# A graph layer on one core: single-row copies taken out, and gathers that land seven to a buffer on counters of their own

## The chip, the cores and the metric

The kernel runs on one core of a Trainium2 chip. The metric is device time of one execution in microseconds (us). TensorE is called PE here, VectorE DVE, ScalarE ACT, GpSimd POOL and SyncE SP, as in the profile. The granted TensorE clock in the profiled execution was 1.000 throughout.

## The reference

There are 50,000 nodes with 128 features each and 1,650,000 edges, sorted by their destination. Each edge takes its source's row through one of two weight matrices, chosen by the edge's type, and the results are summed at the destination.

```python
Xs = X[src]
m_data = Xs @ W_data.T + b_data
m_ctrl = Xs @ W_control.T + b_control
msg = jnp.where((edge_types == 0)[:, None], m_data, m_ctrl)
agg = jax.ops.segment_sum(msg, dst, num_segments=X.shape[0])
out = agg + (X @ W_self.T + b_self)
return jax.nn.relu(out)
...
x = _layernorm(x + _L0_gnn_ref(...), axis=-1)
```

The list of edges holds one self loop per node (source = destination), 50,000 in all; the kernel makes use of that.

## The kernel before

**Order of the sums.** Rows are summed first and multiplied by the weights afterwards. For a block of edges the kernel keeps two sums of source rows per destination node, one for each edge type, in `sums` (a ring of three tiles, each for 128 destination nodes of its own block and the 128 after them). When a block is done, `layer` multiplies the sums of its 128-node window by the two message weights, adds the self term and the biases, and `moments` and `store` do the residual, the layer norm and the output.

**Blocks, steps and chunks.** The sorted edges are cut into blocks of BE = 3800 edges: 28 chunks of 128 edges (C = 28, four steps of R = 7 chunks), 4 x 22 edges that take the place of self loops in those chunks (`fill`, on DVE: a self loop needs no gather, since its row lies in the block's window, so its place in a chunk is given to another edge), and X = 128 edges whose rows are copied one at a time. There are NBLK = 435 blocks. The first has no such extras, and the last has 8 chunks.

**How a row gets to SBUF.** There are two ways.
- `products(b, q)` (line 441) issues on POOL, for each chunk, one indirect DMA that gathers 128 rows of 512 bytes (line 451) into a tile `y` of its own. The pool `gat` holds 70 of these tiles, so POOL can be up to 70 gathers (2.5 blocks) ahead of PE. PE then multiplies `y` by a 128 x 76 matrix of ones and zeros (`oh`, made on DVE by `onehot`, line 396) and so adds each row to the sum of its destination and type: two passes per chunk in float32, line 454. After the 7 chunks of a step (8 in the last step of a block) two small matmuls (line 457) add the counts, and DVE adds the step's result to `sums` (`add`, line 465).
- `single_rows(b, q)` (line 427) copies the X = 128 remaining rows of a block one by one with plain DMAs whose address is in a register: SP issues 64 of them and ACT 64, a quarter of each in each step, two blocks ahead (line 439; the registers are loaded at line 434). They land in one tile `yx`, which is the 29th chunk of the block (k == C in `products`).

**Order on the engines.** The order of all instructions is written out by hand in one Python loop over the blocks (line 520), and each engine works through its share of it in that order. The steps that matter below stand in it as follows.
- At the head of block b DVE adds the last step of block b-1 (line 465), ACT copies the half of `sums` that reaches into the new block (`take_over`, line 470), and DVE adds the left-out self loops (`add_left_out`, line 363).
- In step 1 PE computes the self loops of block b+1 (`left_out_numbers`, line 349). The one PSUM tile `pl` that it writes must have been read by line 363.
- ACT's instructions for block b are `take_over`, one square root (line 489) and the 64 row copies of block b+2, in this order. ACT therefore starts the copy of line 470 for the next block after it has issued the 64 row copies.
- `fill` (lines 297 to 326) works five blocks ahead on DVE and makes the index list `idx` for the gathers. `left_out_columns` (line 333, PE) and `left_out_matrix` (lines 340 and 341, DVE) follow it.

**Waits.** The framework adds all waits. It counts POOL's DMAs on eight counters that take turns. A gather waits until the eighth gather before it has landed, and until PE has used the tile that it overwrites. PE waits for the landing of each gather before its matmul.

If a check of the inputs at the end (lines 569 to 594) found that a step's destinations don't fit its W columns, a slow general version would run; it does not run with these inputs, before or after.

Of the kernel before, what the change touches and what calls it, by code (L numbers as in the profile page):

```python
# [14 lines left out]
U8 = mybir.dt.uint8  # L15
# [8 lines left out]
D = 128  # L24
ROW = 4 * D
# [9 lines left out]
W = 38  # L35
# [3 lines left out]
X = 128  # L39
C1 = C + 1  # L40
F = 22
BE = C * CH + Q * F + X
# [7 lines left out]
GC = GB * C1  # L50
AHEAD = 2
RAHEAD = 5
# [27 lines left out]
def straight(ctx, tc, c, x, x_t, src_t, dst_t, etype_t, src_f, dst_f, etype_f, src_x, dst_first, first_p, out):  # L80

# [18 lines left out]
    gat = ctx.enter_context(tc.tile_pool(name="gat", bufs=70))  # L100
# [49 lines left out]
    one_g = {}  # L150

    def load_edges(g):
        t = eds.tile([1, GB * X], I32, name="one_g")
        nc.sync.dma_start(t, src_x[None, g * GB * X:(g + 1) * GB * X])
        one_g[g] = t
        loads[g] = {}
        for name, a in (("s", src_t), ("d", dst_t), ("t", etype_t)):
            t = eds.tile([P, GB, C1], I32, name=name, bufs=1)
            nc.sync.dma_start(t.rearrange("p b c -> p (b c)"), a[:, g * GC:(g + 1) * GC])
            loads[g][name] = t  # L160
        for name, a in (("sf", src_f), ("df", dst_f), ("tf", etype_f)):
            t = eds.tile([GS, F], I32, name=name, bufs=1)
            nc.sync.dma_start(t, a[g * GS:(g + 1) * GS, :])
            loads[g][name] = t
# [69 lines left out]
    def columns(g):  # L234
# [5 lines left out]
        def first_of(rel, d):  # L240
            yield (rel[:, :, :C].rearrange(steps, r=R), d[:, :, :C].rearrange(steps, r=R),
                   first[:, :, :, None].to_broadcast([P, GB, Q, R]))
            yield rel[:, :, C:], d[:, :, C:], first[:, :, Q - 1:]

        def first_of_f(rel, d):
# [6 lines left out]
        nc.vector.tensor_tensor(h[:, :, :, :R], a["s"][:, :, :C].rearrange(steps, r=R),  # L252
                                a["d"][:, :, :C].rearrange(steps, r=R), op=ALU.is_equal)
# [15 lines left out]
        nc.vector.tensor_scalar(cb, a["t"][:, :, :C], 0.0, float(P), op0=ALU.not_equal, op1=ALU.mult)  # L269
        nc.vector.tensor_tensor(cb, cb, a["d"][:, :, :C], op=ALU.add)  # L270
# [11 lines left out]
        nc.vector.scalar_tensor_tensor(stay, rk, F - LOOP, v[:, :, :C], op0=ALU.is_ge, op1=ALU.mult)  # L282
# [14 lines left out]
    def fill(b):  # L297
# [21 lines left out]
        nc.vector.scalar_tensor_tensor(col_g[g][:, i, :C], idx, -float(P), vi, op0=ALU.mult, op1=ALU.add)  # L319
# [45 lines left out]
    def chunks_of(b, q):  # L365

        n = C1 if not plain(b) else C if b == 0 else RCH if b < NBLK else 0
        return range(q * R, max(q * R, min((q + 1) * R if q < Q - 1 else C1, n)))
# [7 lines left out]
    bys, pcs, zs, pls = {}, {}, {}, {}  # L376
    ats = {}
    ohs, cnts, ys, accs, xws, xTs, pos, hs, mvs, sds = {}, {}, {}, {}, {}, {}, {}, {}, {}, {}
# [5 lines left out]
    def window(b):  # L384
        at = base_of(b)
        xw = stp.tile([B, D], F32, name="xw", bufs=5)
        nc.sync.dma_start(xw, x[bass.ds(at, B), :])
        xT = stp.tile([P, B], F32, name="xT", bufs=5)
        nc.sync.dma_start(xT, x_t[:, bass.ds(at, B)])
        xws[b], xTs[b] = xw, xT  # L390

    def onehot(b):
        g, i = divmod(b, GB)
        n = C1 if not plain(b) else C if b == 0 else RCH
        oh = ohp.tile([P, C1, 2 * W], F32, name="oh")
        nc.vector.tensor_tensor(oh[:, :n, :], col_g[g][:, i, :n, None].to_broadcast([P, n, 2 * W]),  # L396
                                num_ps[:, None, :].to_broadcast([P, n, 2 * W]), op=ALU.is_equal)
        ohs[b] = oh

    def counts(b):  # L400

        cnt = ohp.tile([P, Q, 2 * W], BF16, name="cnt")
        with nc.allow_low_precision(reason="whole numbers up to R + 1"):
            whole = [q for q in range(Q) if len(chunks_of(b, q)) == R]
            n = len(whole)
            nc.vector.tensor_reduce(cnt[:, :n, :], ohs[b][:, :n * R, :].rearrange("p (q r) w -> p q w r", r=R),  # L406
                                    AX.X, ALU.add)
            for q in steps_of(b):
                if q not in whole:
                    k = chunks_of(b, q)  # L410
                    nc.vector.tensor_reduce(cnt[:, q, :], ohs[b][:, k[0]:k[-1] + 1, :].rearrange("p r w -> p w r"),  # L411
                                            AX.X, ALU.add)
        cnts[b] = cnt

    SHARE = X // 2
    TURN = SHARE // Q
    RANGE = dict(min_val=0, max_val=(N - 1) * ROW, skip_runtime_bounds_check_because="where a node's row is")
    x_bytes = x.rearrange("n d -> (n d)").bitcast(U8)[None, :]

    def offsets(b):  # L420

        if not plain(b):
            g, i = divmod(b, GB)
            ats[b] = stp.tile([1, X], I32, name="at_x", bufs=AHEAD + 2)
            nc.vector.tensor_scalar(ats[b], one_g[g][:, i * X:(i + 1) * X], float(ROW), None, op0=ALU.mult)

    def single_rows(b, q):

        if q == 0:
            ys[b] = stp.tile([X, D], F32, name="yx", bufs=AHEAD + 2)  # L430
        both = []
        for j, (eng, dma) in enumerate(((SP, nc.sync), (ACT, nc.scalar))):
            at = j * SHARE + q * TURN
            _, rows = nc.values_load_multi_w_load_instructions(  # L434
                ats[b][0:1, at:at + TURN], engines=[eng], **RANGE)
            both.append([(dma, at + k, row) for k, row in enumerate(rows)])
        for pair in zip(*both):
            for dma, k, row in pair:
                dma.dma_start(ys[b][k:k + 1, :].bitcast(U8), x_bytes[:, bass.ds(row, ROW)])  # L439

    def products(b, q):
        g, i = divmod(b, GB)
        acc = ps.tile([P, 3, W], F32, name="acc")
        ks = chunks_of(b, q)
        for k in ks:
            if k == C:
                r, y = X, ys.pop(b)
            else:
                r = LAST if b == NBLK - 1 and k == RCH - 1 else P
                y = gat.tile([P, D], F32, name="y")  # L450
                nc.gpsimd.indirect_dma_start(  # L451
                    out=y[:r], out_offset=None, in_=x,
                    in_offset=bass.IndirectOffsetOnAxis(ap=idxs[b][:r, k:k + 1], axis=0))
            nc.tensor.matmul(acc[:, :2, :].rearrange("p t w -> p (t w)"), y[:r], ohs[b][:r, k, :],  # L454
                             start=k == ks[0], stop=k == ks[-1])
# [36 lines left out]
    def store(b):  # L492
# [5 lines left out]
        nc.sync.dma_start(out[bass.ds(base_of(b), B), :], o)  # L498

    for b in range(1, AHEAD + 1):  # L500
        offsets(b)
# [7 lines left out]
    for b in range(1, RAHEAD):  # L509
# [3 lines left out]
        if b < AHEAD:  # L513
            onehot(b)
            counts(b)
            for q in range(Q):
                single_rows(b, q)
        if b == 1:
            clear_sums()
    for b in range(NBLK + 1):  # L520
# [16 lines left out]
        for q in range(Q):  # L537
# [24 lines left out]
            if q == 3:  # L562
                left_out_matrix(b + RAHEAD)
                offsets(b + AHEAD + 1)
            if not plain(b + AHEAD):
                single_rows(b + AHEAD, q)
# [252 lines left out]
def gnn_resnorm(  # L819
# [10 lines left out]
    src_x: bass.AP,  # L830
# [39 lines left out]
    with ExitStack() as own:  # L870
        straight(own, tc, c, x, x_t, src_t, dst_t, etype_t, src_f, dst_f, etype_f, src_x,
# [57 lines left out]
```

## Time and profile before

| | before |
|---|---|
| median of 10 runs | 22197.53 us (22146.84 to 22237.11) |
| profiled execution, time | 22200.31 us |
| profiled execution, span | 22198.3 us |
| PE busy, matmuls | 7101.0 us (32%) |
| DVE busy | 6982.5 us (31%) |
| ACT busy | 353.7 us (2%) |
| POOL busy | 11493.4 us (52%) |
| gathers on POOL (line 451) | 12160, mean 945 ns |
| row copies on SP and on ACT (line 439) | 27712 each |

Instructions that issue DMAs from SP and ACT are not counted as busy, so ACT's 2% says nothing about its queue. The idle time of an engine is put down to what ended it. A wait of which the trace doesn't show the source is called "remote", and time in which an engine waited for nothing that the trace shows is called "issue". In the timelines, "ACTq" and "SPq" stand for the queues that issue DMAs, with how many were issued in the stretch shown.

### The profile page before, as it was taken

How to read it: one execution, taken by the hardware profiler on the slowest of the kernel's cores; microseconds unless marked ns; L12 is line 12 of the kernel's file. 1: busy time of each engine (PE TensorE's matmuls, PEld its weight loads, DVE VectorE, ACT ScalarE, POOL GpSimd, SP SyncE). 2: the span in 40 equal slices, each digit the busy share in tenths (PEclk: the TensorE clock that was granted, in tenths of full speed). 3: DMA queues.
4: the chain of work that ended last, by engine and by line, in shares of the span. 5: the costliest groups of instructions: out<-in, count | busy, mean ns of one | idle time of the engine just before them, and what ended most of it. 6: DMA issues, size and time to landing. Idle time of an engine off the chain costs nothing. (4 is left out here: it accounts for less than half of the span.)

```text
span 22198.3 us, 239078 instructions
## 1 busy us (share of the span) xinstructions
PE 7101.0 (32%) x34233; PEld 6718.6 (30%) x34234; DVE 6982.5 (31%) x12861; ACT 353.7 (2%) x875; POOL 11493.4 (52%) x12170
## 2 busy tenths in 40 slices
PE   2333333333333333333333333333333333333333
PEld 2233323333323232323333332233332332332323
DVE  3333333333333333333333333333333333333332
ACT  0000000000000000000000000000000000000000
POOL 5555555555555555555555555555555555555554
DMA  1111111111111111111111111111111111111111
GB/s 47 44 44 44 43 44 44 45 44 44 44 43 44 44 44 44 44 43 45 44 44 43 44 43 44 43 44 43 43 44 43 44 43 44 43 43 44 43 43 37
DMA packets 724493, 968.72 MB, mean 44 GB/s; under 512 B 282786, under 2 KB 522533, under 8 KB 722896
## 3 DMA queue, kind: packets, MB, share of 16 engines
q0 software_dynamic: 389120, 797.69, 13.8%
q1 hardware_dynamic: 277914, 141.12, 2.4%
q10 hardware_dynamic: 55862, 14.50, 0.3%
q14 instruction: 1314, 10.76, 0.2%
q8 instruction: 283, 4.64, 0.1%
HBM read 923.55 MB, written 28.66 MB: 43 GB/s over the span
## 5 line engine op out<-in xcount | busy, mean ns | idle before, releaser
L451 POOL DMA_INDIRECT y<-in_x,idx x12152 | 11484.3, 945 | 10606.6 <-PE acc L454 5659.8
L454 PE MATMUL acc<-oh,y 128*128 128x76 f32 x24320 | 5524.9, 422 | 13.9 <-issue 11.3
L454 PEld LDWEIGHTS acc<-oh,y 128*128 128x128 f32 x24320 | 5365.2, 332 | 14.0 <-issue 14.0
L363 DVE TENSOR_TENSOR sums<-pl,sums 128x384 f32<-128x384 f32 x433 | 241.5, 558 | 12890.5 <-ACT sums L470 12870.6
L349 PE MATMUL pl<-z,ones_b 88*128 88x256 bf16 x433 | 171.0, 395 | 10831.4 <-DVE sums L363 10818.2
L349 PEld LDWEIGHTS <-ones_b 88*128 88x128 bf16 x433 | 45.1, 104 | 10908.8 <-DVE sums L363 10895.5
L406 DVE TENSOR_REDUCE cnt<-oh 128x228 bf16<-128x1596 f32 (+2 forms) x435 | 1278.1, 2938 | 0.1
L333 PE MATMUL small<-ones_b,by 128*88 128x1 bf16 x433 | 100.8, 233 | 3239.3 <-DVE by L326 2614.9
L333 PEld LDWEIGHTS <-by 128*88 128x88 bf16 x433 | 64.0, 148 | 3290.4 <-DVE by L326 2663.9
L396 DVE TENSOR_TENSOR oh<-col,small 128x2204 f32<-128x2204 f32 (+2 forms) x435 | 1049.8, 2413 | 0.0
L457 PEld LDWEIGHTS <-to_row 128*128 128x128 bf16 x3476 | 631.2, 193 | 31.7 <-issue 30.7
L340 DVE COPY at<-small 88x1 f32<-88x1 f32 x433 | 66.9, 155 | 1813.7 <-PE po L475 1112.6
L326 DVE TENSOR_REDUCE by<-old 128x88 bf16<-128x616 f32 x433 | 577.8, 1334 | 19.5 <-issue 1.9
L476 PE MATMUL po<-bias,sums 3*128 3x128 f32 x870 | 344.1, 496 | 701.0 <-DVE sums L465 400.0
L470 ACT COPY sums<-sums 128x384 f32 x434 | 222.2, 512 | 21049.6 <-DMA yx<-in_x 20359.5
L478 PE MATMUL po<-wmsgT,sums 128*128 128x128 f32 x1740 | 531.6, 461 | 0.0
L465 DVE TENSOR_TENSOR sums<-acc,sums 128x114 f32 x1738 | 472.3, 272 | 177.4 <-remote 39.7
L411 DVE TENSOR_REDUCE cnt<-oh 128x76 bf16<-128x608 f32 x434 | 501.4, 1155 | 0.0
L457 PE MATMUL acc<-cnt,to_row 128*128 128x38 bf16 x3476 | 480.8, 219 | 46.1 <-issue 45.4
L476 PEld LDWEIGHTS po<-bias,sums 3*128 3x128 f32 x870 | 216.0, 307 | 824.9 <-DVE sums L465 453.3
L478 PEld LDWEIGHTS po<-wmsgT,sums 128*128 128x128 f32 x1740 | 403.4, 322 | 97.6 <-issue 97.6
L307 DVE TENSOR_TENSOR m<-rk,small 128x616 f32<-128x616 f32 x433 | 344.6, 796 | 17.1 <-DVE small L305 2.4
(116 smaller groups left out, 4524.6 us busy)
## 6 DMA issues: line engine op xcount, KB each, us to landing
yx<-in_x ACTq DMA_DIRECT2D x27712, 0.5 KB
yx<-in_x SPq DMA_DIRECT2D x27712, 0.5 KB
y<-in_x,idx POOLq DMA_INDIRECT x12152
xw<-in_x SPq DMA_DIRECT2D x435, 64.0 KB
xT<-in_x_t SPq DMA_DIRECT2D x435, 64.0 KB
out<-o SPq DMA_DIRECT2D x435, 64.0 KB
vf_all<-vd SPq DMA_DIRECT2D x44, 440.0 KB
s<-in_src_t SPq DMA_DIRECT2D x44, 145.0 KB
```

The costliest lines, as they stand in the source:

```text
L307: nc.vector.tensor_tensor(m, rk_g[g][:, i, :, None].to_broadcast([P, C, F]), rank_no_ps[:, None, :].to_broadcast([P, C, F]), op=ALU.is_equal)
L326: nc.vector.tensor_reduce(by, old.rearrange("p (q r) f -> p q f r", r=R), AX.X, ALU.add)
L363: nc.vector.tensor_tensor(part, pls.pop(b)[:, :, :B], part, op=ALU.add)
L396: nc.vector.tensor_tensor(oh[:, :n, :], col_g[g][:, i, :n, None].to_broadcast([P, n, 2 * W]), num_ps[:, None, :].to_broadcast([P, n, 2 * W ...
L406: nc.vector.tensor_reduce(cnt[:, :n, :], ohs[b][:, :n * R, :].rearrange("p (q r) w -> p q w r", r=R), AX.X, ALU.add)
L411: nc.vector.tensor_reduce(cnt[:, q, :], ohs[b][:, k[0]:k[-1] + 1, :].rearrange("p r w -> p w r"), AX.X, ALU.add)
L451: nc.gpsimd.indirect_dma_start(out=y[:r], out_offset=None, in_=x, in_offset=bass.IndirectOffsetOnAxis(ap=idxs[b][:r, k:k + 1], axis=0))
L454: nc.tensor.matmul(acc[:, :2, :].rearrange("p t w -> p (t w)"), y[:r], ohs[b][:r, k, :], start=k == ks[0], stop=k == ks[-1])
L457: nc.tensor.matmul(acc[:, 2, :], to_row[:, t, :], cnts[b][:, q, t * W:(t + 1) * W], start=t == 0, stop=t == 1)
L465: nc.vector.tensor_tensor(part, accs.pop((b, q)), part, op=ALU.add)
L476: nc.tensor.matmul(po, a[0:3, 2, :B], bias, start=False, stop=False)
L478: nc.tensor.matmul(po, a[:, t, :B], c["wmsgT"][:, t * D:(t + 1) * D], start=False, stop=t == 1)
```

## The change

The single rows go. A block has BE = 28 x 128 + 88 = 3672 edges, the number of blocks becomes 450, the last with 11 chunks, and the number of gathers goes from 12160 to 448 x 28 + 28 + 11 = 12583. The functions `offsets` and `single_rows`, the lists of single rows and their loads go with them. W goes from 38 to 36, so that `oh` has 28 x 72 numbers per partition in place of 29 x 76.

The gathers of a step go into one tile `y` of seven slots. The pool has ten of these tiles, so the room is 70 gathers as before. Each tile has a completion counter of its own. The framework's eight counters are not used for these gathers, and PE waits once per step, until all seven have landed. The address for the output of a block is no longer loaded a second time (`bases`).

```diff
-W = 38
+W = 36
-X = 128
-C1 = C + 1
-BE = C * CH + Q * F + X
+BE = C * CH + Q * F
+SLOTS = 10
...
-    gat = ctx.enter_context(tc.tile_pool(name="gat", bufs=70))
+    gat = ctx.enter_context(tc.tile_pool(name="gat", bufs=SLOTS))
...
-    def offsets(b):
...
-    def single_rows(b, q):
...
+    landed = [tc.alloc_semaphore(f"landed{i}") for i in range(SLOTS)]
+    seen = [0] * SLOTS
+    step_no = [0]
+
+    def gathers(b, q):
+        ks = chunks_of(b, q)
+        i = step_no[0] % SLOTS
+        step_no[0] += 1
+        y = gat.tile([P, R, D], F32, name="y")
+        for k in ks:
+            r = LAST if b == NBLK - 1 and k == RCH - 1 else P
+            copy = nc.gpsimd.indirect_dma_start(
+                out=y[:r, k - ks[0], :], out_offset=None, in_=x,
+                in_offset=bass.IndirectOffsetOnAxis(ap=idxs[b][:r, k:k + 1], axis=0))
+            copy.then_inc(landed[i], 16)
+            tc.no_tile_sem_insts.add(copy.ins.name)
+            tc.add_to_no_dep_group(f"rows{b}_{q}", copy.ins)
+        seen[i] += 16 * len(ks)
+        wait = nc.tensor.wait_ge(landed[i], seen[i])
+        tc.declare_fence(wait.ins, group=f"rows{b}_{q}")
+        return y
 
     def products(b, q):
+        y = gathers(b, q)
...
-            if k == C:
-                r, y = X, ys.pop(b)
-            else:
-                r = LAST if b == NBLK - 1 and k == RCH - 1 else P
-                y = gat.tile([P, D], F32, name="y")
-                nc.gpsimd.indirect_dma_start(
-                    out=y[:r], out_offset=None, in_=x,
-                    in_offset=bass.IndirectOffsetOnAxis(ap=idxs[b][:r, k:k + 1], axis=0))
-            nc.tensor.matmul(acc[:, :2, :].rearrange("p t w -> p (t w)"), y[:r], ohs[b][:r, k, :],
+            r = LAST if b == NBLK - 1 and k == RCH - 1 else P
+            nc.tensor.matmul(acc[:, :2, :].rearrange("p t w -> p (t w)"), y[:r, k - ks[0], :], ohs[b][:r, k, :],
                              start=k == ks[0], stop=k == ks[-1])
...
-        nc.sync.dma_start(out[bass.ds(base_of(b), B), :], o)
+        nc.sync.dma_start(out[bass.ds(bases.pop(b), B), :], o)
...
-                offsets(b + AHEAD + 1)
-            if not plain(b + AHEAD):
-                single_rows(b + AHEAD, q)
```

## The prediction

> **What bounds the kernel now.** I read the page first. It shows no engine near full: POOL leads with 52%, and nearly half of its span is idle. The costliest group is the gather.
>
> ```profile
> POOL 5555555555555555555555555555555555555554
> L451 POOL DMA_INDIRECT y<-in_x,idx x12152 | 11484.3, 945 | 10606.6 <-PE acc L454 5659.8
> yx<-in_x ACTq DMA_DIRECT2D x27712, 0.5 KB
> ```
>
> The load is the same from end to end, so one block stands for all: 22198.3 / 435 = 51.03 us. Next I read the list of waits, which shows who holds whom.
>
> ```profile
> ACT sums L470 <- DMA yx<-in_x: 20359.5, 418, 175.6
> DVE sums L363 <- ACT sums L470: 12870.6, 432, 40.8
> PE pl L349 <- DVE sums L363: 10818.2, 431, 34.6
> POOL y L451 <- PE acc L454: 5674.1, 1326, 19.5
> POOL y L451 <- issue: 2806.7, 8949, 3.9
> POOL y L451 <- remote: 1491.6, 1281, 6.1
> ```
>
> Read it from the bottom up. POOL waits for PE's matmul of line 454 (the matmul 70 gathers back frees its tile). PE waits 25 us a block (10818.2 / 431) at line 349 for DVE's line 363, DVE waits 30 us for ACT's copy of line 470, and ACT is not waiting for data at all: it is issuing row copies. ACT's timeline says so.
>
> ```profile
> 9989.99 0.51 ACT L470 COPY sums<-sums 128x384 f32 x1 [51.28 <-DMA xw<-in_x]
> 9992.25 0.29 ACT L489 ACTIVATE sd<-mv,eps 128x1 f32<-128x1 f32 x1 [1.75 <-DVE mv L487]
> 9993.46 46.64 ACTq L439 DMA_DIRECT2D yx<-in_x  x64
> 10040.92 0.51 ACT L470 COPY sums<-sums 128x384 f32 x1 [48.38 <-DMA xw<-in_x]
> ```
>
> From one copy of line 470 to the next are 50.93 us, and 46.64 of them go into 64 row copies (0.73 us each). That is the block's period. What hangs on it is seen right after 10040.92 in the timeline of all engines:
>
> ```profile
> 10041.47 0.56 DVE L363 TENSOR_TENSOR sums<-pl,sums 128x384 f32<-128x384 f32 x1 [27.64 <-ACT sums L470]
> 10042.08 0.39 PE L349 MATMUL pl<-z,ones_b 88*128 88x256 bf16 x1 [23.29 <-DVE sums L363]
> 10042.48 3.21 PE L454 MATMUL acc<-oh,y 128*128 128x76 f32 x14
> 10043.41 0.94 POOL L451 DMA_INDIRECT y<-in_x,idx  x1 [10.87 <-PE acc L454]
> ```
>
> ACT, DVE, PE and POOL start within 2.5 us of each other. ACT's queue of row copies is the bound, and POOL is held by it through four hands. What POOL does when nobody holds it is seen at the start, where the 70 tiles are still free:
>
> ```profile
> 102.14 0.94 POOL L451 DMA_INDIRECT y<-in_x,idx  x1 [0.30 <-issue]
> 103.38 0.94 POOL L451 DMA_INDIRECT y<-in_x,idx  x1 [0.30 <-issue]
> 104.63 0.94 POOL L451 DMA_INDIRECT y<-in_x,idx  x1 [0.30 <-issue]
> 106.25 0.94 POOL L451 DMA_INDIRECT y<-in_x,idx  x1 [0.67 <-PE acc L454]
> ```
>
> One gather per 1.248 us: from 32.23 to 104.63 in the same timeline are 58 gathers in 72.40 us. The first wait for a tile comes after some 78 of them. Finally, the end of the trace, where ACT has no more rows to issue:
>
> ```profile
> 22146.73 0.51 ACT L470 COPY sums<-sums 128x384 f32 x1 [34.09 <-DMA yx<-in_x]
> 22155.55 0.51 ACT L470 COPY sums<-sums 128x384 f32 x1 [6.26 <-DVE sums L465]
> 22170.86 0.51 ACT L470 COPY sums<-sums 128x384 f32 x1 [8.89 <-DVE sums L465]
> ```
>
> The same copies are now 8.82 and 15.31 us apart, and they wait for DVE instead of the row copies.
>
> **The change part by part.**
>
> *Row copies removed.* ACT and SP lose 64 copies and their register loads in each block, ACT the 46.64 us seen above. ACT keeps 0.51 + 0.29 us of work a block, and line 470 starts as soon as DVE's line 465 is done. How soon is that? The trace has it: from line 470 to the line 465 that the next line 470 needs are 20.65 us (5009.15 to 5029.80), 22.1 (5059.69 to 5081.80), 23.6 (9989.99 to 10013.55) and 24.0 (18057.33 to 18081.30). So the loop of ACT, DVE and PE could turn in about 20 to 24 us per block. This includes DVE's wait at line 340, whose six rows sum to 1814 us or 4.2 us a block.
>
> *What is late next.* POOL. A block needs 28 gathers, and 28 x 1.2486 = 34.96 us, against 24 for the loop. (1.2486 is the mean duration 0.9450, which is 11484.3 / 12152, plus the gap of 0.3036 between two unhindered ones.) The margin is 11 us a block, and every tenth block's `columns` uses up some 6 us of it on DVE (24.4 to 30.6 in the start's timeline). PE and DVE then wait for the gathers, and the tiles that POOL wants are long free.
>
> *More blocks.* The 128 edges of each block that went by row copies go by gathers: 12583 in place of 12160. The 423 more cost 423 x 1.2486 = 528 us on the path. The 15 more blocks of DVE and PE work lie beside POOL's.
>
> *Counters of their own.* Each gather loses a wait on POOL's queue (an EVENT_SEMAPHORE of 17 ns, 12092 of them). I count nothing for it: the first of these waits is at 39.8 us, and the gathers before it stand at the same 0.30 us from each other as those after it. If POOL waits instead once a step for a tile or a counter, a bound from above is 0.2 us x 1800 steps = 360 us, worked out from the 0.12 us per gather that the "remote" waits take now (1491.6 / 12152), rounded up. Below zero I allow 0.02 us per gather, the EVENT_SEMAPHORE itself: -0.25 ms at most, in the main case nothing.
>
> *One wait of PE for seven.* PE starts a step up to six gathers (7.5 us) later than it could. Behind that wait stand the step's matmuls, then DVE's line 465. POOL is at least 60 gathers from needing those tiles, so it costs nothing but once, at the end.
>
> *W from 38 to 36, the 29th chunk gone.* DVE's `oh` and `cnt` shrink (2.42 us and 1.15 us in a block of the trace), PE saves a chunk per block. All of it lies beside POOL. SP no longer loads an address twice; SP binds nothing.
>
> *A rule weighed: sharing out descriptor work.* The row is the 46.64 us for 64 copies. The Trainium skill ("Perfetto Trace Analysis", DMA Optimizations) advises spreading DMAs over SP, ACT and GpSimd where generating descriptors is the bottleneck. By it this change is a loss: POOL takes 528 us more and nothing comes back, some 22,730 us. But the trace has 128 rows in 1.25 us on POOL and one row in 0.73 us on ACT, with the pass to the next block behind it. The rows decide; I follow them.
>
> *A second rule: DVE against POOL.* The row is the gather's mean of 945 ns with a median of 944: stretching costs about 13 us in the whole run. Some of it is at the start, where a gather took 2.41 us beside DVE's long operations. The skill ("SBUF — State Buffer", SBUF: two separate sides) says that GpSimd can't write descriptors while DVE runs an operation in a two-port mode. DVE's busy share rises from 31% to about 44% of the time, so each gather would meet more of them: its copies, casts and scalar operations come to about 1.4 us a block (lines 304, 305, 318, 340, 341, 497), at worst 450 x 1.4 = 630 us. The trace's 13 us already contain the same operations per block, so I take 15 us and keep half of the rule's figure in the range.
>
> *The sum.* Start of the first gather 8.3, stretching of the first gathers about 4, then 12583 x 1.2486 = 15,711. After the last gather comes a tail: the last product to the end took 22.4 us before (22175.9 to 22198.3), plus landing, and some 10 us because the last block is short (11 gathers, 13.7 us) and the loop of 20 us lags: 35 us. Span: 8 + 4 + 15,711 + 35 = 15,758 us. The time is 2.0 us over the span, as in the profiled execution before, whose 22200.31 is 2.8 us above the median: 15,760 us.
>
> **The rivals.**
>
> *A: POOL unheld, as above.* For it: the four hands, the first 78 gathers, the end of the trace. 15,760 us.
>
> *B: the loop of DVE, PE and ACT becomes the bound.* In the window 5009.15 to 5059.69 DVE is busy 15.43 us, PE 16.18, ACT 0.81, together 32.4; with the 4.2 us at line 340 it would be 36.6 us a block if nothing overlapped: 450 x 36.6 = 16,470 us. It decides from 34.96 us. Against it: the 20 to 24 us measured.
>
> *C: a gather waits for PE's one wait of the step before (slower).* All gathers of a step count on one tile's counter, and the fence for tile and counter is on PE. If the fence makes POOL hold the next step's first gather until PE is through with the last one, then a step is 8.74 us of gathers, about 3.3 us of matmuls and a landing. No row here shows a landing; the skill ("DMA: Bandwidth & Descriptors", Anatomy of one DMA) puts 2.0 us plus bytes over 436 GB/s, 2.15 us as an estimate. 14.2 us x 1800 = 25,560 us. It turns into a loss from 12.3 us a step (22,198 / 1800), a stall of 3.6 us. Against it: ten tiles and ten counters.
>
> *D: ACT only looks like the bound.* If POOL kept its 1.8255 us per gather (22198.3 / 12160) for another reason, 12583 of them give 22,970 us. Against it: the end of the trace.
>
> **How the numbers follow.** A 0.88, B 0.09, C 0.02, D 0.01. The time is A's, 15,760. The low end, 15,650, is A without its tail and with a third of the EVENT_SEMAPHOREs' time given back. The high end adds to A the 360 us of new waits or half of the 630, and reaches into B's lower part: 16,150. A and B are faster, C and D slower: faster 0.965, slower 0.03, and 0.005 for within 0.2%, about what a measurement of this kernel can tell from no change.
>
> **What would show it.** POOL's busy share near 75% with nearly all its idle time under "issue", a spacing of 1.25 us everywhere; ACT idle ended by DVE's line 465, not by DMAs; PE's largest wait for gathers, about 18 us a block. Wrong would be: POOL still waiting for PE for microseconds in each block (B or C; a wait in every step for C, in every block for B), or a gather clearly longer than 945 ns.

## The result: 0.813 of the time in the first measurement, and 1.028 on another chip

| | kernel before | kernel after | ratio, 95% |
|---|---|---|---|
| first measurement | 22192.25 us (28 runs) | 18051.33 us (8 runs, 18048.51 to 18053.09) | 0.8134 [0.8127, 0.8141] |
| a second chip, both kernels unchanged | 15339.33 us (7 runs, 15279.42 to 15342.36) | 15759.26 us (4 runs, 15757.71 to 15760.01) | 1.028 [1.0256, 1.0304] |

The prediction was 15,760 us and a range of 15,650 to 16,150. The first measurement is outside of it, though on the predicted side. On the second chip the predicted time came out within a microsecond, but there the kernel before is faster still, and the change is a loss. Both rows have to be explained. The experiments ran on four chips. The kernel before took 22,131 us on the first of them, within 0.4% of the profile that the prediction was made from, and 15,242 to 15,339 us on the other three. Below, "first chip" stands for the first measurement and the first four experiments, which agree in what is compared here (the record doesn't say whether they shared one chip); "quick chips" are the other three.

The profiled execution of the kernel after in the first measurement took 18052.87 us, with a span of 18051.2. Lines of its page:

```profile
POOL 6666666666666666666666666666666666666665
L417 POOL DMA_INDIRECT y<-in_x,idx x12572 | 11909.5, 947 | 6067.4 <-issue 3581.6
L434 PE MATMUL acc<-oh,y 128*128 128x72 f32 x25166 | 6026.4, 408 | 3808.3 <-issue 3786.4
L445 DVE TENSOR_TENSOR sums<-acc,sums 128x108 f32 x1798 | 482.1, 268 | 7234.6 <-remote 6551.1
```

The row copies are gone, and a gather still takes 947 ns. POOL's idle time fell from 10606.6 to 6067.4 us, but only 3581.6 of it is the 0.30 us behind every gather ("issue"). About 2,490 us are waits, 5.5 us in each of 450 blocks, and 18051.2 / 450 = 40.1 us a block is some 5 us more than the 34.96 that the gathers need. The list of waits names who is late:

```profile
DVE sums L445 <- remote: 6551.1, 594, 19.7
ACT sums L450 <- DVE sums L445: 5276.1, 288, 31.5
PE acc L434 <- issue: 3786.4, 3340, 3.3
DVE h L463 <- remote: 2263.8, 323, 13.8
POOL y L417 <- remote: 1403.8, 540, 6.2
```

ACT now waits for DVE, as predicted, and no longer for DMAs. But DVE waits up to 19.7 us for something that the trace can't name, and PE loses 3786 us to "issue", which hardly existed before (11.3 us on the same kind of product). The timeline shows what is behind both words:

```profile
10022.78 3.24 PE L434 MATMUL acc<-oh,y 128*128 128x72 f32 x14
...
10027.34 1.22 PE L458 MATMUL po<-wmsgT,sums 128*128 128x128 f32 x4
...
10034.95 0.28 PE L434 MATMUL acc<-oh,y 128*128 128x72 f32 x1 [1.84 <-issue]
...
10036.36 0.28 PE L434 MATMUL acc<-oh,y 128*128 128x72 f32 x1 [1.13 <-issue]
...
10039.17 0.27 DVE L445 TENSOR_TENSOR sums<-acc,sums 128x108 f32 x1 [14.19 <-remote]
...
10047.65 0.29 DVE L463 SCALAR_TENSOR_TENSOR h<-po,xw 128x128 f32<-128x128 f32 x1 [8.20 <-remote]
...
10049.32 3.23 PE L434 MATMUL acc<-oh,y 128*128 128x72 f32 x14
...
10049.45 0.95 POOL L417 DMA_INDIRECT y<-in_x,idx  x1 [3.71 <-remote]
```

The products of step 0 are recorded from 10022.78 to 10026.02, yet DVE, whose addition waits in the program for PE's tick behind them (what PE adds to a counter when it is done), starts its addition at 10039.17, 13 us after their recorded end. `layer`'s products are recorded as done at 10028.6, and DVE's line 463 starts at 10047.65, 19 us later. The counter's own events in the trace say the same: PE's counter has none from 10022.78 to 10037.04, then one at 10039.15 and one at 10047.62, just ahead of DVE's two starts. So PE's records run ahead of what PE reports as done. Whether the products themselves come late or only their report, the trace doesn't tell; "PE is late" stands for both below. Behind it PE's next matmuls trickle in one at a time, their starts multiples of 0.70 us apart (10034.95, 10036.36), where 14 of them take 3.24 us at full pace. At 10049.32 all is fast again: POOL stood still, after 10044.80, until 10049.45.

Is PE late because the rows land late? No. POOL's last gathers before another of its pauses start at 10002.28 and 10003.54, and after them the DMAs fall silent. The DMA view of the window 10007 to 10009.5, in which POOL waits for a tile until 10009.49:

```profile
DMA packets 0, 0.00 MB, mean 0 GB/s; under 512 B 0, under 2 KB 0, under 8 KB 0
```

Everything that was issued has landed, and POOL waits all the same. How far POOL is ahead of PE is told by counting, from the windows view: 6978 gathers had started by 9985 us, and 13846 passes of products (two to a chunk).

```profile
0.00:9985.00 9985.00, 6612.02 (x6978) 1.00 0.20 54
```

```profile
0.00:9985.00 9985.00, 3319.00 (x13846) 3175.36 (x13846) 1.00 0.20 54
```

6978 - 13846 / 2 = 55 chunks, in a ring of 70 whose tiles are given back seven at a time, and only when PE's tick is there. POOL has run ahead as far as it may, and is held by PE.

**The same kernel on the second chip.** The same lines of its page and list of waits:

```profile
POOL 7777777777777777777777777777777777777777
L417 POOL DMA_INDIRECT y<-in_x,idx x12572 | 11877.6, 945 | 3830.6 <-issue 3829.5
L434 PE MATMUL acc<-oh,y 128*128 128x72 f32 x25166 | 5811.8, 424 | 8089.6 <-PEq L424 8089.5
L445 DVE TENSOR_TENSOR sums<-acc,sums 128x108 f32 x1798 | 486.9, 271 | 6366.5 <-PE acc L437 6294.0
```

```profile
ACT sums L450 <- DVE sums L445: 10882.4, 449, 83.9
PE acc L434 <- PEq L424: 8089.5, 1783, 7.5
POOL y L417 <- issue: 3832.9, 12580, 0.3
DVE h L463 <- PE po L458: 997.0, 450, 2.2
```

This is the profile that the prediction described. All of POOL's idle time is "issue", 0.30 us each; PE waits at line 424 for the gathers, 8089.5 / 450 = 18.0 us a block; nothing is "remote". By 10000 us 7996 gathers and 15975 / 2 product pairs have started: PE is 8 or 9 chunks behind POOL in place of 55.

**The kernel before on the two chips.** The prediction's bound was 46.64 us for 64 row copies of ACT. On the second chip, from one copy of line 470 to the next:

```profile
10030.62 0.51 ACT L470 COPY sums<-sums 128x384 f32 x1 [34.98 <-DMA yx<-in_x]
10032.89 0.30 ACT L489 ACTIVATE sd<-mv,eps 128x1 f32<-128x1 f32 x1 [1.75 <-DVE mv L487]
10034.10 30.49 ACTq L439 DMA_DIRECT2D yx<-in_x  x64
10065.40 0.51 ACT L470 COPY sums<-sums 128x384 f32 x1 [32.22 <-DMA yx<-in_x]
```

The same 64 copies take 30.49 us, 0.48 each. From one copy of line 470 to the next are 34.78 us, and 28 gathers take 34.96: ACT's turn and POOL's are level. In the page of the kernel before there:

```profile
L451 POOL DMA_INDIRECT y<-in_x,idx x12152 | 11484.5, 945 | 3756.3 <-issue 2086.2
DMA 44%; ACTq 21%; issue 11%; SPq 11%; PE 7%; DVE 5%; ACT 1%; DVEq 0%; POOL 0%; POOLq 0%
```

POOL's idle time is 3756.3 / 12152 = 0.309 us a gather, hardly more than the 0.305 of the kernel after, so POOL runs at its own pace. But the second line, the shares of the chain that ended last, still names the row copies and their queues and not POOL. The two bounds stand side by side, so taking the copies away frees nothing.

Why is a row copy 0.73 us on one chip and 0.48 on the other? The view of line 439 gives minimum, median and maximum of every instruction on it, in ns. The first chip:

```profile
L439 ACTq MOVE yx<-in_x x27712: 2/29/1422, 25.0 to 22145.6; - x200
```

and the second:

```profile
L439 ACTq MOVE yx<-in_x x27712: 29/29/29, 25.5 to 15278.7; - x200
```

This MOVE only puts an address into a register of ACT. On the second chip all 27712 take 29 ns. On the first one the median is the same, but some are held up for as long as 1422 ns. When? I took the time from the last start of a gather to each MOVE in the first chip's trace of the kernel before, and the share of MOVEs that took over twice the median:

| since the last gather's start | ACT's MOVEs held up | SP's MOVEs held up |
|---|---|---|
| 0 to 1.3 us | 12.4% of 19733 | 31.1% of 15637 |
| 1.3 to 2.5 us | 26.9% of 1493 | 26.2% of 1806 |
| 2.5 to 4 us | 3.2% of 1574 | 2.3% of 3188 |
| 4 to 6 us | 0.1% of 1678 | 0.1% of 1368 |
| over 6 us | 0.0% of 3234 | 0.0% of 5713 |

On the first chip ACT's and SP's queues are held up while a gather is under way, and not otherwise. A whole row copy of ACT, from one MOVE to the next, tells it too: 0.75 us on average within 2.5 us of a gather's start, 0.41 us after more than 4 us, and 0.42 us on the second chip. Most of the MOVEs held up took about 0.70 us (2270 of ACT's 2898 lie between 0.65 and 0.75), the same step in which PE's matmuls trickle in. PE's trickle also has the same pattern, fast when POOL pauses.

The hold-up grows while POOL gathers without a break, that is, with no more than 2 us between two starts. Within 1.3 us of a gather's start, 1.3% of ACT's MOVEs are held up in the first 4 us of such a stretch, 15.9% from 4 to 8 us, 44.5% from 8 to 12 and 72.6% from 12 to 20 (SP: 23.0, 31.4, 55.7 and 85.3%). In the kernel before, a stretch is 7 gathers long on average; in the kernel after, again on the first chip, it is 17.

There the change takes the queue with 128 such copies off the path (and the 46.64 us with it), and leaves PE's lateness. On the second chip's traces there is nothing of either, and the change only adds gathers.

### The profile page after: what moved, and what is told of

Same layout as the page of the kernel before. It is cut to its first block, busy times and chain, and to the rows that moved or that the text cites. A ratio compares the mean times of both kernels' runs of the same rounds, so it can differ in the third digit from the quotient of the medians.

```text
span 18051.2 us, 112758 instructions
## 1 busy us (share of the span) xinstructions
PE 7608.5 (42%) x34521; PEld 7004.9 (39%) x34522; DVE 6881.7 (38%) x12350; ACT 366.0 (2%) x905; POOL 11921.4 (66%) x12593
## 4 chain that ended last, share of the span: by engine, by line
another core or an unknown queue 49%; issue 23%; DVE 20%; PE 7%; DVEq 1%; ACT 0%; DMA 0%; ACTq 0%; SPq 0%
PE acc L434 5%; DVE by L316 3%; DVE m L297 2%; DVE new L300 2%; DVE v_new L304 2%; DVE sums L445 2%; DVE old L313 2%; DVE pl L348 1%; PE po L458 1%; DVE o L477 1%; DVE sums L353 1%; DVE st L465 1%; DVE h L463 1%; DVE z L331 1%
## 5 line engine op out<-in xcount | busy, mean ns | idle before, releaser
L417 POOL DMA_INDIRECT y<-in_x,idx x12572 | 11909.5, 947 | 6067.4 <-issue 3581.6
L434 PE MATMUL acc<-oh,y 128*128 128x72 f32 x25166 | 6026.4, 408 | 3808.3 <-issue 3786.4
L434 PEld LDWEIGHTS acc<-oh,y 128*128 128x128 f32 x25166 | 5770.6, 325 | 4095.0 <-issue 4051.7
L445 DVE TENSOR_TENSOR sums<-acc,sums 128x108 f32 x1798 | 482.1, 268 | 7234.6 <-remote 6551.1
L323 PE MATMUL small<-ones_b,by 128*88 128x1 bf16 x448 | 104.0, 232 | 4661.1 <-DVE by L316 3511.3
L395 DVE TENSOR_REDUCE cnt<-oh 128x288 bf16<-128x2016 f32 x450 | 1674.0, 3720 | 0.1
L463 DVE SCALAR_TENSOR_TENSOR h<-po,xw 128x128 f32<-128x128 f32 x450 | 130.8, 291 | 2518.3 <-remote 2263.8
L385 DVE TENSOR_TENSOR oh<-col,small 128x2016 f32<-128x2016 f32 x450 | 998.4, 2219 | 0.0
L437 PE MATMUL acc<-cnt,to_row 128*128 128x36 bf16 x3596 | 498.4, 215 | 356.2 <-issue 355.8
L342 PE MATMUL pl<-z,to_row 88*128 88x128 bf16 x896 | 221.4, 288 | 714.4 <-issue 714.4
L300 DVE TENSOR_TENSOR new<-m,small 128x616 f32<-128x616 f32 x448 | 356.3, 795 | 16.3 <-DVE m L297 1.1
L304 DVE TENSOR_REDUCE v_new<-new 128x28 f32<-128x616 f32 x448 | 356.1, 795 | 16.3 <-issue 0.6
```

The costliest lines, as they stand in the source:

```text
L300: nc.vector.tensor_tensor(new.rearrange("p (q r) f -> p q r f", r=R), m.rearrange("p (q r) f -> p q r f", r=R), vf.rearrange("p (q f) -> p ...
L304: nc.vector.tensor_reduce(v, new, AX.X, ALU.add)
L417: copy = nc.gpsimd.indirect_dma_start(out=y[:r, k - ks[0], :], out_offset=None, in_=x, in_offset=bass.IndirectOffsetOnAxis(ap=idxs[b][:r, ...
L437: nc.tensor.matmul(acc[:, 2, :], to_row[:, t, :], cnts[b][:, q, t * W:(t + 1) * W], start=t == 0, stop=t == 1)
L445: nc.vector.tensor_tensor(part, accs.pop((b, q)), part, op=ALU.add)
```

## The experiments

The theories that were weighed, by the letters of the expectations (which are not the prediction's A to D): **S**, each PE instruction costs more beside gathers. **K**, PE is slow when it starts from idle. **C**, what PE finishes comes at a fixed rate, however little work it has. **H**, the form of C that was left after one_gather: what PE finishes is held up while gathers are under way. **R**, PE's reading of the row tiles collides with the gathers' writing. **G**, a gather lands only every 18051.2 / 12583 = 1.43 us. **P**, the chip sets the pace of ACT's copies and of PE.

### First chip: one part alone (old_counters)

```diff
-    gat = ctx.enter_context(tc.tile_pool(name="gat", bufs=SLOTS))
+    gat = ctx.enter_context(tc.tile_pool(name="gat", bufs=70))
...
-        y = gathers(b, q)
...
+            y = gat.tile([P, D], F32, name="y")
+            nc.gpsimd.indirect_dma_start(out=y[:r], out_offset=None, in_=x, ...)
```

> The single rows are out, but each gather has a tile of its own and the framework's eight counters, as before the change. Everything measured in the kernel after stays the same otherwise (12583 gathers, W = 36). If taking out the rows is what made the kernel faster and the new bound is PE, whose instructions are the same: 18,050 us within 300. If the new counters brought a part of the gain: 18,500 us or more, with POOL waits under 'remote' that come from the eight counters. If POOL's waits for a whole tile of seven cost something: below 17,800.

18036.33 us (4 runs) beside 22131.29 for the kernel before, ratio 0.8153 [0.8136, 0.817]. The row copies' removal makes all of the gain. Counters of their own and one wait for seven change no more than 0.1% (18051.33 us with them).

### First chip: half the passes of PE (half_passes)

```diff
-            nc.tensor.matmul(acc[...], y[:r, k - ks[0], :], ohs[b][:r, k, :],
+            nc.tensor.matmul(acc[...], y[:r, k - ks[0], :].bitcast(BF16)[:, 1::2],
+                             ohs[b][:r, k, :].bitcast(BF16)[:, 1::2],
```

The products see the upper 16 bits of each number, which makes them one pass in bf16.

> The products read only the upper 16 bits of each float32 (rows and ones alike, every second bfloat16 of the same bytes), so PE runs one load of weights and one matmul per chunk in place of two and two: about 101 PE instructions a block in place of 157. DVE, POOL and the waits are unchanged; the sums are rounded to bfloat16. Theory S (while gathers land, each PE instruction takes about 0.6 us, otherwise 0.12): PE keeps up much better, 15,800 to 16,500 us. Theory C (PE's completion count climbs at about 0.9 us a tick, the ticks being unchanged): 18,050 within 200. Theory K (PE is slow for some 20 us after each idle stretch, whatever it runs): 17,500 to 18,050.

17817.74 us (one run): 12583 products and weight loads fewer, and 1.3% less time. DVE waits for PE as in the kernel after:

```profile
L446 DVE TENSOR_TENSOR sums<-acc,sums 128x108 f32 x1798 | 483.4, 269 | 5229.7 <-remote 4686.0
```

A price that every PE instruction pays beside gathers (S: 15,800 to 16,500 us) is out. C misses its range of 18,050 within 200 by a little, and the time lies in K's.

### First chip: most gathers left out (one_gather)

```diff
-        ks = chunks_of(b, q)
+        ks = chunks_of(b, q)[:1]
...
-            nc.tensor.matmul(acc[...], y[:r, k - ks[0], :], ohs[b][:r, k, :],
+            nc.tensor.matmul(acc[...], y[:r, 0, :], ohs[b][:r, k, :],
```

One gather a step in place of seven; all seven products read its rows, so the sums are of other rows.

> Only the first of the seven gathers of a step is issued, and all seven matmuls of the step read its slot, so the sums are of the wrong rows. PE's and DVE's instructions stay. POOL's load falls from 28 gathers a block to 4, so the loop of DVE, PE and ACT alone sets the pace. Theory S: PE runs at full speed nearly all the time, 20 to 24 us a block, 9,000 to 10,800 us. Theory C: the count climbs as before, 40 us a block, 18,000. Theory K: PE still idles while it waits for DVE's fill and is slow after it, 14,000 to 18,000.

9156.9 us, 20.3 us a block, in S's range; C (18,000 us) and K are out here. So PE's lateness needs the gathers, and of C only H is left. In the page PE's products wait for nothing:

```profile
L434 PE MATMUL acc<-oh,y 128*128 128x72 f32 x25166 | 5701.9, 421 | 10.9
```

With 4 gathers a block the loop of DVE, PE and ACT turns on the first chip in 20.3 us, inside the prediction's 20 to 24. So its 40.1 us in the kernel after come from running beside 28.

The same pair of traces speaks against R. `layer`'s products read `sums`, the weights and the bias, and none of the row tiles. In one_gather DVE's line 463 waits 2.2 us for them in each block (997.0 us in 450 times, as on the second chip). In the kernel after the same wait is 5.6 us on average (2518.3 us in 450 blocks), 13.8 at most. DVE's wait before it is for step 0's products, which PE finishes earlier, so what it waits for here is `layer`'s products (in 330 of its 358 waits over 1 us an event of PE's counter stands just ahead of DVE's start), and they are late without reading the tiles.

### First chip: more work for PE (busy_pe)

```diff
         if not plain(b):
+            junk = ps_o.tile([B, D], F32, name="po")
+            for _ in range(40):
+                nc.tensor.matmul(junk, ones_b, ones_b, start=True, stop=True)
             pc = sums_at[b % 2]
```

> 40 more matmuls of ones a block, into a PSUM tile that nobody reads, just ahead of line 323, where PE idles some 9 us a block. Theory S: up to 80 more PE instructions a block at 0.25 to 0.6 us each, 22,000 us or more. Theory C: no more ticks, 18,050 within 300. Theory K: PE doesn't idle there and stays fast, 15,800 to 16,500 us.

18161.73 us (one run), 0.6% more with 40 more matmuls and weight loads a block, inside C's range. Neither S (it should cost far more) nor K stands: PE's wait for DVE at this place fell from 3511.3 us in the kernel after to 45.6, and the time is no shorter. H was left, with R and G as rivals; the DMA view above speaks against G, and `layer`'s products against R.

### A quick chip: what PE reads, how much it does, how much is gathered

Four kernels that were meant to tell H, R and G apart ran once each on the second chip, where the kernel before took 15324.02 us beside them. unread lets the products read a constant tile:

```diff
+    still = keep.tile([P, D], F32, name="still")
+    nc.vector.memset(still, 1.0)
...
-            nc.tensor.matmul(acc[...], y[:r, k - ks[0], :], ohs[b][:r, k, :],
+            nc.tensor.matmul(acc[...], still[:r, :], ohs[b][:r, k, :],
```

> All gathers and PE's wait for their landing stay; the 7 products of a step read one constant tile in place of the gathered rows (so the output holds none of them). Theory H (what PE finishes is held back while gathers are being issued, whatever PE reads): 18,050 us or more, with DVE still waiting 10 us and longer for products whose records ended long before. Theory R (PE's reading of the row tiles collides with the gathers' writing into the same tiles): POOL's own pace, 28 x 1.2486 = 34.96 us a block, 15,700 to 15,900 us. Theory G (the rows land only every 1.43 us): 18,050 us, with PE waiting for landing counters.

15758.89 us. one_product keeps the gathers and drops 6 of 7 products:

```diff
+            if k == ks[-1]:
-            nc.tensor.matmul(..., start=k == ks[0], stop=k == ks[-1])
+                nc.tensor.matmul(..., start=True, stop=True)
```

> All 7 gathers of a step stay with PE's wait for all of them; only the last chunk's product is run (6 of 7 chunks are left out of the sums). Theory H with a price for each PE instruction that has to finish beside gathers: PE has 24 products fewer a block, so POOL's pace, 15,700 to 16,100 us. Theory H with a price that doesn't follow PE's work (PE held until the gathers pause): 17,500 to 18,050 us. Theory G: 18,050 us.

15780.65 us. Taken alone, the first would have shown R and the second a price by PE's instructions. They show neither, since the unchanged kernel after takes 15759.26 us on that chip: there was no lateness to take away. four_of_seven issues 4 gathers of 7:

```diff
-        for k in ks:
+        for k in ks[:4]:
...
-            nc.tensor.matmul(acc[...], y[:r, k - ks[0], :], ohs[b][:r, k, :],
+            nc.tensor.matmul(acc[...], y[:r, min(k - ks[0], 3), :], ohs[b][:r, k, :],
```

> Only 4 of a step's 7 gathers are issued, 16 a block in place of 28; the 7 products stay and read those 4 chunks (the other rows are left out of the sums). POOL's own pace is then 16 x 1.2486 = 19.98 us a block, the loop of DVE, PE and ACT with few gathers about it was 20.3 us. Theory H (each gather holds PE's completions back): on the line between 4 gathers a block (20.3 us) and 28 (40.1 us), 0.825 us a gather, 30.2 us a block, 13,600 us. Theory G (1.4346 us a gather): 22.95 us a block, 10,330 us. If neither gathers nor landing slow PE: 9,200 to 9,500 us.

9168.05 us, 20.4 us a block, next to the range for "neither gathers nor landing slow PE". POOL needs 19.98 and the loop 20.3; with 16 gathers a block beside it the loop is as quick here as with 4 on the first chip. half_rows fetches 64 rows a gather, and its products run over 64 rows (the same edit in both places):

```diff
-            r = LAST if b == NBLK - 1 and k == RCH - 1 else P
+            r = 64
```

> Each gather fetches 64 rows in place of 128, and each product runs over 64 rows (the other half of the edges is left out); the number of gathers, products, waits and ticks stays. Theory H with a price for each gather's issue: 18,050 us if the issue of a gather still takes 1.25 us. With a price for each descriptor or row (theory H by rows, theory G by bytes): half of the stall at least goes, 15,700 to 16,900 us; if POOL's own time for a gather falls with the rows too, down to 9,500 us.

15244.06 us, below the 15,700 to 16,900 expected for less work per row. Its gathers, from the view of line 417, take 903 ns at the median:

```profile
L417 POOL DMA_INDIRECT y<-in_x,idx x12572: 899/903/3027, 8.4 to 15199.1; - x200
```

Half the rows save 42 ns of 945. A gather's price on POOL is nearly all for the instruction.

### A quick chip: both kernels unchanged (before_again, after_again, unread_again)

After that one low time of the kernel before, both kernels ran unchanged.

> The kernel before, unchanged, once more, with a profile. In the call of the runs without a reader its one time was 15,324 us, where all earlier ones were 22,067 to 22,237. Theory P (the chip that a call gets, or its condition, sets the pace of ACT's row copies and of PE): 22,100 to 22,200 us with 0.73 us for each row copy of ACT on a chip like the first ones, or 15,320 us with at most 35.3 us for ACT's 64 copies of a block, POOL without waits for PE. Theory F (that one time was a freak): 22,100 to 22,200 us again.

> The kernel after, unchanged, on the same chip as the others of this call. Theory P: 18,050 us where the kernel before takes 22,150; where the kernel before takes 15,320 it takes POOL's pace, 15,750 to 15,790 us, and is 2.8% slower. Theory F: 18,050 us.

15333.49 us for the kernel before, with 30.49 us for ACT's 64 copies in the timeline above, and 15759.26 for the kernel after: P, in both figures. The low time was no freak. unread ran beside them as a third, with the expectation

> The kernel whose products read a constant tile in place of the gathered rows, once more. If the kernel after takes 18,050 us in this call: theory R (reading the row tiles collides with the gathers' writing) 15,760 us, theory H (PE is held back beside gathers whatever it reads) 18,000 us or more. If the kernel after takes 15,760 us in this call, 15,760 us, and the earlier run of it tells nothing of PE.

and took 15764.12 us.

### A third chip: the two parts apart where nothing holds POOL (rows_kept, old_counters_2)

rows_kept is the kernel before with `gathers` of the kernel after, for the chunks below C:

```diff
+        slot = gathers(b, q)
...
             if k == C:
                 r, y = X, ys.pop(b)
...
-                y = gat.tile([P, D], F32, name="y")
-                nc.gpsimd.indirect_dma_start(out=y[:r], out_offset=None, in_=x, ...)
+                y = slot[:, k - ks[0], :]
```

> The kernel before with its single rows kept, and only the gathers' counters and PE's one wait for a step taken over from the change. Theory P (POOL's pace where ACT's row copies are quick: a gather's issue 0.945 us and 0.315 us of idle in the kernel before, 0.304 us with counters of its own): 12,160 gathers x 1.2486 and about 40 us, 15,190 to 15,260 us, ratio 0.992 to 0.996, where the kernel before takes 15,340; 22,050 to 22,250 us, no gain, where the kernel before takes 22,150, since ACT's copies hold POOL there. Theory W (one wait for seven gathers delays PE): slower than the kernel before by 0.5% or more.

> The single rows taken out, but every gather in a tile of its own under the framework's counters. Theory P: where the kernel before takes 15,340 us, 12,583 gathers x (0.945 + 0.315) = 15,855 us and a tail, 15,850 to 15,920 us, ratio 1.034 to 1.038; where it takes 22,150, 18,036 us again, ratio 0.815. If the framework's counters cost POOL nothing: 15,760 us, ratio 1.028.

The kernel before took 15242.48 us (13 runs), 0.6% less than on the second chip. rows_kept: 15238.99 us (10 runs), ratio 0.9998 [0.9988, 1.0007]: the counters and the one wait give nothing and cost nothing. The time is in P's range and the ratio is not, since the kernel before was quicker than expected. old_counters_2: 15783.22 us (4 runs), ratio 1.0355 [1.0338, 1.0373]. Its time misses P's range, and its ratio lies in it only because the kernel before was quicker as well. The whole loss lies with the single rows: 423 gathers more at 1.2486 us are 528 us, and 15783.22 - 15242.48 = 541 were measured. My higher figure for the framework's counters took 0.315 us of idle time a gather as their price; in old_counters_2 it is 0.305 (3831.6 us for 12572). With a single run of unread on this chip,

> The kernel whose products read a constant tile, once more. Where the kernel before takes 22,150 us: theory R (reading the row tiles collides with the gathers' writing) 15,760 us, theory H (PE is held back beside gathers whatever it reads) 18,000 us or more. Where the kernel before takes 15,340 us: 15,760 us, which tells nothing of PE.

15774.57 us.

### A fourth chip (unread_4, one_product_2, half_rows_2)

The three kernels that ask about PE's lateness ran once more, each a single time.

> Products read a constant tile in place of the gathered rows. Where the kernel before takes 22,150 us: theory R (reading the row tiles collides with the gathers' writing) 15,760 us, theory H (PE is held back beside gathers whatever it reads) 18,000 us or more. Where the kernel before takes 15,240 to 15,340 us: 15,760 us.

> All gathers, but only one product a step in place of seven (6 of 7 chunks are left out of the sums). Where the kernel before takes 22,150 us: 15,780 us if PE's lateness follows the number of products that it has to finish beside gathers, 17,500 us or more if it does not. Where the kernel before takes 15,240 to 15,340 us: 15,780 us.

> Each gather fetches 64 rows in place of 128 (the other half of the edges is left out), numbers of instructions unchanged. Where the kernel before takes 22,150 us: 17,400 us or more if PE's lateness follows the number of gathers, 15,240 to 16,500 us if it follows the rows or bytes that they move. Where the kernel before takes 15,240 to 15,340 us: 15,240 us.

The kernel before took 15322.92 us beside them: again a quick chip, and about the same times again, 15758.2, 15784.08 and 15291.57 us. None of the three ran on the first chip, so whether PE's lateness there follows the rows that the gathers move, or their number, stays untried.

No kernel here was shown to beat both on every chip. On the first chip half_passes was the quickest of those that issue all gathers, with fewer bits in its products. On the third chip rows_kept equals the kernel before, 3.4% below old_counters_2.

## Why the prediction was right or wrong

- **The step that failed: "the tiles that POOL wants are long free".** On the first chip they are not. PE reports its products 13 to 19 us after their records end (in the block shown), POOL is 55 chunks ahead of PE's recorded starts, and it is held for 5 us a block. 40.1 us a block in place of 34.96, times 450, are the 2,300 us that the time lies over the prediction. The words that the prediction named as its failure, "POOL still waiting for PE for microseconds in each block", are what the profile shows. It assigned them to its rivals B or C.
- **B's place was right, its price and its reason were not.** The loop does become the bound on the first chip, but its own work did not grow: with 4 gathers a block it takes 20.3 us there. It is held up beside the gathers. The prediction took "about 20 to 24 us per block" from the kernel before, where POOL stands still for 16 us of every block (51.03 - 34.96), and carried it over to a kernel in which POOL would not stand still. Even the four turns that it read hold 13, 14, 15 and 15 starts of gathers, where POOL's pace would give 17 to 19. With stretches of 17 gathers in place of 7 the hold-up has time to grow, as counted under the table. That this growth is what takes the turn from 24 to 40 us is argued; no run on the first chip set the length of the stretches alone. A sign was in the page, and the prediction even added it up: 4.2 us a block at line 340, where DVE waits for one small matmul of line 333. The page of the kernel before puts that wait down to the wrong matmul on the first chip (first line below), to the right one on the second (second line), and there it is 13 times shorter.

```profile
L340 DVE COPY at<-small 88x1 f32<-88x1 f32 x433 | 66.9, 155 | 1813.7 <-PE po L475 1112.6
```

```profile
L340 DVE COPY at<-small 88x1 f32<-88x1 f32 x433 | 66.9, 154 | 140.7 <-PE small L333 139.7 <-issue 1.0
```

- **"ACT's queue of row copies is the bound"** was right for the trace it was read from: taking the copies out, alone, gave the whole gain (0.8153). As a property of the kernel it was wrong. A copy is 0.73 us only where gathers hold ACT's queue up; on the second chip it is 0.48, ACT's turn is no longer than POOL's, and the gain is not there to be had.
- **The sum itself** held where nothing holds PE up: 12583 x 1.2486 and 35 us of tail against 15759.26 us. Start (8.37) and PE's wait (18.0 us a block) are as written. That it agrees within a microsecond is in part luck: the last gather starts at 15728.85, 7 us later than in the sum, and the end (15756.0) follows 9 us sooner after it.
- **528 us for 423 gathers** was right as the price of the gathers: 541 us on the third chip. On the second the loss was only 420 us (15759.26 - 15339.33), since the kernel before takes 97 us more there than on the third.
- **The 360 us for new waits of POOL** were called a bound from above, and were none: 0.12 us a gather is 0.86 us for each step of seven. No such wait came, so nothing hung on it.
- **The first rule weighed**, spreading DMAs over the engines, was set aside for the row. On the quick chips the rule is right: there ACT and SP copy 128 rows a block beside POOL's gathers without adding to the time (rows_kept, and the kernel before), and the change gives these to POOL. The prediction's 22,730 us for it was worked out from the slow pace.
- **The second rule**, DVE holding up descriptor writing, cost next to nothing: a gather's mean stayed at 945 to 947 ns, at most 25 us in all, with DVE busy 38 and 44% of the time in place of 31%.
- **C did not happen**: rows_kept has the same counters and fence as the change, and its ratio is 0.9998.

What stays open: why one chip of four holds up ACT, SP and PE beside gathers. That ACT's and SP's moves are held up only within some 4 us of a gather is shown. That PE is late only beside many gathers is shown by one_gather. That both are the same thing is argued, from the pauses and from the common step of 0.70 us. No kernel with as many gathers, but of fewer rows or with products that read none of them, ran on that chip.

One rival is untested: the recording of the profile. Where 28 gathers a block run on the first chip, the traces hold only about half of the counter events of DVE (5506 of 9877 in the kernel after); in one_gather they hold 9875, and on the second chip 9860. So the recording, too, falls short there beside the gathers. The record lists a span beside the time of nearly every execution, so they seem to have been recorded in the same way, and no run tells whether the hold-up would be there without it.

## What to carry to other kernels

Before you call a queue the bound, look at its cheapest instruction: a register move that takes 29 ns at the median and 1422 at most says that something else holds the queue up, and that its price may not be there on another chip. A loop that was timed while its partner paused has not been timed beside a partner that doesn't pause. Time a change on more than one chip when its gain rests on such a price; here the same two kernels gave 0.813 and 1.028. And don't take PE's recorded ends for its completions: where an engine starts long after the records of all that it waits for, count how far the producer is ahead of the consumer.

## What the runs showed of the hardware

- On one of the four chips of the experiments the queues of ACT and SP were held up, by as much as 1.4 us an instruction, within about 4 us of a gather's start, and hardly ever later (table above), and the more so the longer POOL had gathered without a break (1.3% to 72.6% of ACT's moves). PE's matmuls trickled in at multiples of 0.70 us there while POOL gathered. POOL's own pace, 1.25 us a gather, was the same on all of them.
- A gather of 64 rows takes POOL 903 ns, one of 128 rows 945. From these two, an estimate: about 0.86 us for the instruction and 0.7 ns a row.
- Half-size products (one bf16 pass in place of two in float32) and 80 further PE instructions a block moved the time by 1.3% and 0.6%, while the granted clock in those two runs was 0.54 and 0.51 in place of 1.0. In the second of them 14 float32 products take 3.24 us at full pace, as in the kernel after with its 1.0. (The traces with 1.0 hold no record of a change of the clock.)
